# Four sums of blocks of h, made by Pool instead of VectorE

## The chip, the cores and the metric

One core of a Trainium2 chip runs the whole program. The metric is the time of one execution on the device in microseconds (us), as the median of several runs. Engines are named as in the profile: PE is TensorE, PEld its weight loads, DVE is VectorE, ACT is ScalarE, POOL is GpSimd (called Pool here), SP is SyncE, which here issues most of the DMAs.

## What is computed

The reference normalizes x (2048 tokens by 1024), and adds to x a convolution along the hidden dimension (the S4 part) and a gated feed-forward with 4-bit weights. Cut to the part that the change lies in:

```python
xn = layernorm(x)
g = einsum('bsh,ih->bsi', xn, dequantize(gate_Wq, gate_scale, gate_zero))
u = einsum('bsh,ih->bsi', xn, dequantize(up_Wq, up_scale, up_zero))
h = silu(g) * u                       # 2048 tokens x 2752
ffn = einsum('bsi,hi->bsh', h, dequantize(down_Wq, down_scale, down_zero))
out = x + s4(xn) + ffn
```

Each int4 weight is a nibble minus a zero, times a scale, with one zero and one scale for each 64 inputs.

## The kernel before

The matrix products are made by a scheme of the Strassen-Winograd kind: a 2 by 2 block product takes 7 smaller products instead of 8, for sums and differences of blocks that VectorE makes beforehand. Each fp32 operand is split into a high and a low fp16 half, and a product has three passes over these halves (`PASS`, line 530).

The program has three stages.

**Start, up to about 165 us.** x is loaded and normalized token tile by token tile (`norm_stat`, `norm_hi`, `norm_lo`), the blocks of x are combined (`combine`), and the first two of 21 tiles of the inner dimension (j = 0 and 1, 128 rows each) are multiplied plainly (`gate_up_plain`). Many steps of VectorE, ScalarE and SP are pinned here: they run in the order in which they are written (class `Engine`, line 66).

**Gate/up products, to about 888 us.** For j = 2 to 20 and two halves of the tokens (`cp`), `gate_up` makes seven products of 12 matmuls of 512 columns into the PSUM banks A, B, C and D. In between, ScalarE and VectorE evacuate banks: `hb` is C copied and later D added (line 599), `ha` is C copied and B added (lines 602 to 606). Two of the seven products of a group are put off into the next group (`pending`). At the end of `third`, `finish_h` is called with `ha` and `hb`, the blocks of h for the two token halves in `cp`.

Beside these products run two more flows. `load_w` makes the weights of a later j: SP loads `raw` and `sz`, VectorE unpacks the nibbles into `w`, Pool prepares scales and offsets (`scale_c`, lines 290 to 295, three small instructions), ScalarE scales 64 columns at a time, VectorE makes sums (`sums`), ScalarE and VectorE write the high and low fp16 halves into `nat`, and SP transposes `nat` into `wf`, which the matmuls read. `load_wd` does the like for the down weights and stores them to DRAM in seven combinations (`nd` to `WD`), with scales fetched from `SZT`. A smaller flow computes the S4 kernel (tiles `s4n`, `s4p`).

**Convolution and down product, to the end.** The last stage reads the blocks of h (`HF`) and of the down weights (`WD`) from DRAM and multiplies them (line 1187). It is not touched by the change.

`finish_h` is where the change is. For an even j it stores `ha` to `HF[0]` and keeps both tiles as s0 and s2 in `slots`. For the odd j that follows it stores `ha` and `hb` as s1 and s3, and makes four sums of [128 x 512] fp32 tiles in SBUF: s4 = s0 − s2, then s2 = s2 + s3, s0 = s2 − s0, and s6 = s1 − s0. Each is stored to its place in `HF` by a DMA that SP issues (`emit`, line 642). In the trace the tile names are those at allocation, so that s0 and s1 are `ha`, s2 and s3 are `hb`, and s4 and s6 are `s` (for j = 0 and 1, `h` in place of `ha` and `hb`). There are 10 odd j below 20 and two values of `cp`, so 20 calls make 80 sums. The tiles come from the pool "h" (4 buffers under the tag "h" for odd j, 4 under "e" for even j), and a buffer is free again when the DMA that reads it has landed.

The order on each engine comes from two sources. Where a step is pinned, from the code:

```python
            if self.last is None:
                self.last = method(*args, **kw)
            else:
                with self.tc.issue_after(self.last.ins):
                    self.last = method(*args, **kw)
```

Elsewhere a planner (`schedule_with_timeline_sim=True`, line 1370) simulates the program with its own estimates of times, and fixes the order of each engine's instructions by them, and the places of the waits. `G`, Pool's handle, is never pinned (line 115). On the chip each engine and SP's queue issue in the order so fixed.

Of the kernel before, what the change touches and what calls it, by code (L numbers as in the profile page):

```python
# [29 lines left out]
ALU = mybir.AluOpType  # L30
# [57 lines left out]
def build(nc, tc, x, xp, raw_d, sz_d, par_d, vct_d, tab_d, csrow_d, out):  # L88
# [3 lines left out]
    with es:  # L92
# [15 lines left out]
        def htile(name, tag="h"):  # L108
            return pools["h"].tile([P, 512], F32, tag=tag, name=name)
# [4 lines left out]
        V, A = Engine(tc, nc.vector), Engine(tc, nc.scalar)  # L114
        SP, G, PE = Engine(tc, nc.sync), nc.gpsimd, nc.tensor
# [18 lines left out]
        def wtemp(kind, shape, dtype, name):  # L134
            return home[kind].tile(shape, dtype, tag=kind, name=name, **({"bufs": szbufs[0]} if kind == "sz" else {}))
# [14 lines left out]
        def split(dst, src):  # L150

            A.copy(dst[:, 0], src)
            V.tensor_tensor(dst[:, 1], src, dst[:, 0], ALU.subtract)
# [104 lines left out]
        with ea:  # L258
# [11 lines left out]
            def unpack(gi):  # L270

                if gi in FETCH:
                    with tc.issue_after(rs[FETCH[gi], 0].ins):
                        rawt[gi] = load_raw(gi)
                raw, sz = load_raw(gi) if gi not in rawt else rawt.pop(gi)
                w = wtemp("w", [P, 7, 256], F32, f"w{gi}")
                wv = w.rearrange("p a b -> p (a b)")[:, 0:1024]
                q = wv.bitcast(I32).rearrange("p (a b c) -> p a b c", a=16, b=2)
                V.tensor_scalar(q[:, :, 0, :], raw, 4, 15, ALU.logical_shift_right, ALU.bitwise_and)
                V.tensor_scalar(q[:, :, 1, :], raw, 15, None, ALU.bitwise_and)  # L280
                return w, sz
# [280 lines left out]
            def gate_up(j, cp, wf):  # L562
# [46 lines left out]
                def third(ha):  # L609
                    prod(3, bD, False, True)  # L610
                    A.activation(bD, bD, AF.Silu, scale=isc)
                    V.scalar_tensor_tensor(hb, hb, HS * isc, bD, mult, mult)
                    finish_h(j, cp, ha, hb)
# [20 lines left out]
            def finish_h(j, cp, ha, hb):  # L634
                nm = f"{j}_{cp}"
                if j == NJ - 1:
                    for c, h in enumerate((ha, hb)):
                        pc = wtemp("nat", [P, 2, 512], F16, f"hpl{nm}_{c}")
                        split(pc, h)
                        A.dma_start(HPL[cp][:, c, 0:2, :], pc)  # L640
                    return
                def emit(f, src):
                    SP.dma_start(HF[cp][f, :, j // 2, :], src)

                if j % 2 == 0:
                    emit(0, ha)
                    slots[cp] = (ha, hb)
                    return
                s0, s2 = slots.pop(cp)
                s1, s3 = ha, hb  # L650
                s4, s6 = (htile(f"s{n}_{nm}") for n in (4, 6))
                emit(1, s1)
                emit(3, s3)
                V.tensor_tensor(s4, s0, s2, ALU.subtract)
                emit(4, s4)
                V.tensor_tensor(s2, s2, s3, ALU.add)
                emit(2, s2)
                V.tensor_tensor(s0, s2, s0, ALU.subtract)
                emit(5, s0)
                V.tensor_tensor(s6, s1, s0, ALU.subtract)  # L660
                emit(6, s6)


# [171 lines left out]
            w0, s0 = unpack(0)  # L835
            w1, s1 = unpack(1)
# [25 lines left out]
            w2, s2 = unpack(2)  # L862
# [12 lines left out]
            w3, s3 = unpack(3)  # L875
# [41 lines left out]
            h1a = gate_up_plain(1, 0, 0, wt[1])  # L917
            mix_h(0, 1, mix(0, 1))
            finish_h(0, 0, h0a, gate_up_plain(0, 0, 1, wt[0]))
            norms("H8", "S9", "L8", "H9", "S10", "L9", "H10", "S11", "L10", "H11", "S12", "L11")  # L920
            fetch(13)
# [9 lines left out]
            run(t0, 1)  # L931
            norms("L15")
            finish_h(1, 0, h1a, gate_up_plain(1, 0, 1, wt[1]))
            run(t0)
            keep_x(0)
# [438 lines left out]
```

## Time and profile before

| | |
|---|---|
| median of 3 runs | 1339.83 us (1339.01 to 1342.43) |
| the profiled execution | 1342.33 us, span 1340.6 us |
| mean granted TensorE clock in it | 0.989 |
| busy: PE, DVE, ACT, POOL | 1267.3, 992.3, 664.6, 193.1 us |
| the four sums in the stage of gate/up products (190 to 870 us) | 72 instructions, 49.4 us on DVE |

The span runs from the first to the last instruction of the profiled execution; its own time has some 1.7 us more around it. A line of a group gives the line of the kernel, the engine, the operation, the tiles written and read, their shapes, the count, then the busy time in us and the mean of one in ns, and after the bar the idle time of the engine just before them with what ended it. L77 and L82 are lines of the helper that issues most instructions, so that instructions are told apart by their tiles. A line of waits gives who waited for whom, the total in us, how many times, and the longest. A row of the timeline gives the start, the duration, the engine and the instruction; rows of several merged instructions end in their count.

### The profile page before, as it was taken

How to read it: one execution, taken by the hardware profiler on the slowest of the kernel's cores; microseconds unless marked ns; L12 is line 12 of the kernel's file. 1: busy time of each engine (PE TensorE's matmuls, PEld its weight loads, DVE VectorE, ACT ScalarE, POOL GpSimd, SP SyncE). 2: the span in 40 equal slices, each digit the busy share in tenths (PEclk: the TensorE clock that was granted, in tenths of full speed). 3: DMA queues.
4: the chain of work that ended last, by engine and by line, in shares of the span. 5: the costliest groups of instructions: out<-in, count | busy, mean ns of one | idle time of the engine just before them, and what ended most of it. 6: DMA issues, size and time to landing. Idle time of an engine off the chain costs nothing.

```text
span 1340.6 us, 20432 instructions
## 1 busy us (share of the span) xinstructions
PE 1267.3 (95%) x7664; PEld 739.2 (55%) x7664; DVE 992.3 (74%) x1337; ACT 664.6 (50%) x1183; POOL 193.1 (14%) x262
## 2 busy tenths in 40 slices
PE   3799999999989998989989999999999999999998
PEld 3344444444434444434434444455567888888887
DVE  7579966487788769687868776653738897788792
ACT  5468457655736475576648646620204433443330
POOL 4320001000010001000100100000000022255540
PEclk9899999999999999999989999999999999999999
DMA  9993967487799797969869994966837679799991
GB/s 228 210 240 93 195 169 158 104 206 215 181 252 224 175 226 185 266 140 280 221 172 230 209 272 106 242 208 201 332 127 293 247 201 273 246 258 266 288 188 51
DMA packets 377279, 280.72 MB, mean 209 GB/s; under 512 B 230548, under 2 KB 323548, under 8 KB 373084
## 3 DMA queue, kind: packets, MB, share of 16 engines
q1 hardware_dynamic: 354556, 266.31, 72.8%
q0 software_dynamic: 21760, 10.49, 6.6%
q10 hardware_dynamic: 864, 2.62, 0.5%
q8 instruction: 60, 0.98, 0.3%
q14 instruction: 39, 0.32, 0.1%
HBM read 132.36 MB, written 94.84 MB: 169 GB/s over the span
## 4 chain that ended last, share of the span: by engine, by line
PE 40%; DVE 6%; DMA 4%; ACT 2%; issue 2%; SPq 1%; DVEq 0%; ACTq 0%
PE A L1187 14%; PE D L1187 7%; PE cv L1091 5%; PE E L1187 3%; PE cv L1113 3%; DVE w L77 2%; PE D L569 2%; PE A L569 2%; DMA w<-SZT 2%; PE C L569 2%; SPq L77 1%; PE B L569 1%; ACT w L77 1%; PE cc L1126 1%; DMA raw<-qn 1%
## 5 line engine op out<-in xcount | busy, mean ns | idle before, releaser
L569 PEld LDWEIGHTS <-wf 128*128 128x128 f16 x3192 | 313.3, 98 | 418.9 <-issue 43.0
L1187 PEld LDWEIGHTS <-g 128*128 128x128 f16 x2940 | 287.6, 98 | 33.5 <-issue 0.2
L77 ACT ACTIVATE w<-w,sz 128x64 f32<-128x64 int32 x640 | 217.3, 427 | 70.6 <-DVE w L77 66.5
L569 PE MATMUL D<-x,wf 128*128 128x512 f16 x912 | 215.9, 385 | 16.4 <-DVE hb L77 11.9
L569 PE MATMUL A<-x,wf 128*128 128x512 f16 x912 | 213.4, 381 | 10.8 <-DMA wf<-nat 5.5
L569 PE MATMUL C<-x,wf 128*128 128x512 f16 x912 | 207.8, 379 | 2.8 <-DVE ha L77 1.5
L77 ACT CAST g<-a 128x2560 f16<-128x2560 f32 x42 | 97.5, 2324 | 183.2 <-PE cv L1113 53.5
L77 DVE TENSOR_TENSOR w<-w 128x256 f32<-128x256 f32 (+2 forms) x272 | 139.5, 528 | 64.7 <-ACT w L77 56.0
L1187 PE MATMUL A<-b,g 128*128 128x256 f16 x1680 | 185.9, 273 | 0.0
L77 DVE TENSOR_TENSOR g<-a,g 128x2560 f16<-128x2560 f32 x42 | 118.4, 2821 | 30.9 <-ACT g L77 30.9
L1226 POOL DMA_DIRECT2D out<-o x64 | 78.8, 2183 | 340.0 <-DVE o L77 329.7
L292 POOL TENSOR_SCALAR sz<-sz 128x16 f32<-128x16 f32 x41 | 18.5, 451 | 680.8 <-DMA sz<-in_sz 658.5
L569 PE MATMUL B<-x,wf 128*128 128x512 f16 x456 | 107.2, 385 | 2.1 <-ACT B L77 2.1
L538 PEld LDWEIGHTS <-wf 128*128 128x128 f16 x624 | 58.3, 107 | 89.5 <-DMA wf<-natp 30.6
L77 ACT CAST nat<-w 128x896 f16<-128x896 f32 x76 | 68.2, 935 | 72.8 <-issue 51.9
L1187 PE MATMUL D<-b,g 128*128 128x256 f16 x840 | 94.0, 273 | 0.0
L77 DVE TENSOR_TENSOR nat<-w,nat 128x896 f16<-128x896 f32 x76 | 80.3, 1086 | 13.9 <-ACT nat L77 13.8
L77 ACT CAST nd<-w 128x896 f16<-128x896 f32 x70 | 63.3, 935 | 45.6 <-DVE w L77 29.0
L538 PE MATMUL g<-x,wf 128*128 128x512 f16 (+1 forms) x264 | 49.0, 348 | 31.5 <-DMA wf<-natp 27.9
L77 DVE TENSOR_TENSOR nd<-w,nd 128x896 f16<-128x896 f32 x70 | 74.8, 1084 | 2.4 <-ACT nd L77 2.3
L1091 PEld LDWEIGHTS <-x 128*128 128x128 f16 x576 | 52.7, 98 | 25.5 <-issue 4.3
L77 DVE SCALAR_TENSOR_TENSOR p<-cv,p 128x512 f32<-128x512 f32 x32 | 21.9, 689 | 50.5 <-PE cv L1113 45.5
(144 smaller groups left out, 1243.5 us busy)
## 6 DMA issues: line engine op xcount, KB each, us to landing
a<-HF SPq DMA_DIRECT2D x28, 1280.0 KB, 7.9
WD<-nd SPq DMA_DIRECT2D x70, 448.0 KB, 4.2
b<-WD SPq DMA_DIRECT2D x49, 640.0 KB, 6.2
w<-SZT SPq DMA_DIRECT2D x80, 256.0 KB, 5.8
raw<-in_raw SPq DMA_DIRECT2D x65, 256.0 KB, 3.4
HF<-ha SPq DMA_DIRECT2D x54, 256.0 KB, 3.0
HF<-s SPq DMA_DIRECT2D x40, 256.0 KB, 3.2
HF<-hb SPq DMA_DIRECT2D x36, 256.0 KB, 2.6
```

The costliest lines, as they stand in the source:

```text
L77: return method(*args, **kw)
L292: G.tensor_scalar(sz[:, 0], sz[:, 0], WS, None, ALU.mult)
L538: PE.matmul(ps[:, ts], w(k, wi), xt[k // 4][:, xi, k % 4, ts], start=(k == 0 and n == 0), stop=(k == 7 and n == 2))
L569: ends[0] = PE.matmul(ps, wf[kt // 2][:, 14 * (kt % 2) + 2 * fa + wi, :], xt[:, xi, kt, :], start=(start and kt == 0 and n == 0), stop=(st ...
L1091: PE.matmul(dst, w, m, start=first[0], stop=False, skip_group_check=True)
L1113: mm = lambda w, m, stop=False: PE.matmul(ps, w, m, start=False, stop=stop, skip_group_check=True)
L1126: PE.matmul(pc[:, 0:256], xs[:, c, xi, k, ts], band[:, bi, 512 - P * k : 768 - P * k], start=(k == 0 and n == 0), stop=(k == 1 and n == 2))
L1187: PE.matmul(dst, g[:, i, hi, ts], b[:, i, :, wi, :], start=(new and q + i + n == 0), stop=(q == 1 and i == half - 1 and n == 2), skip_grou ...
L1226: G.dma_start(dst, o[:, q], accum_op=ALU.add)
```

## The change

The four sums in `finish_h` are issued on Pool (`G`) instead of VectorE (`V`). Their operands, their order in the code and the stores after them stay as they are.

```diff
@@ -651,13 +651,13 @@
                 s4, s6 = (htile(f"s{n}_{nm}") for n in (4, 6))
                 emit(1, s1)
                 emit(3, s3)
-                V.tensor_tensor(s4, s0, s2, ALU.subtract)
+                G.tensor_tensor(s4, s0, s2, ALU.subtract)
                 emit(4, s4)
-                V.tensor_tensor(s2, s2, s3, ALU.add)
+                G.tensor_tensor(s2, s2, s3, ALU.add)
                 emit(2, s2)
-                V.tensor_tensor(s0, s2, s0, ALU.subtract)
+                G.tensor_tensor(s0, s2, s0, ALU.subtract)
                 emit(5, s0)
-                V.tensor_tensor(s6, s1, s0, ALU.subtract)
+                G.tensor_tensor(s6, s1, s0, ALU.subtract)
                 emit(6, s6)
```

## The prediction

> **What bounds the kernel now.** I read the page first, then the stage that the change touches as one window, then TensorE's waits in that window, then VectorE's groups and SP's waits in it, and last single rows of Pool and VectorE side by side.
>
> ```profile
> span 1340.6 us, 20432 instructions
> ...
> PE 1267.3 (95%) x7664; PEld 739.2 (55%) x7664; DVE 992.3 (74%) x1337; ACT 664.6 (50%) x1183; POOL 193.1 (14%) x262
> ```
>
> TensorE is busy for 95% of the span and nobody else is near it. The sums lie in the stage of gate/up products. Its steady part, 190 to 870 us, as one window (the columns are PE, PEld, DVE, ACT, POOL, clock, DMA share, GB/s):
>
> ```profile
> 190.00:870.00 680.00, 647.88 (x2989) 291.21 (x2988) 510.11 (x856) 419.07 (x914) 54.22 (x102) 0.98 0.81 204
> ```
>
> TensorE stands idle for 680 − 647.9 = 32.1 us of it. No change to VectorE's load can bring more than that, while nothing limits what it can cost. VectorE has 75% of the window, Pool 8%. What TensorE's idle time ended on there (total, times, longest; the first fence is matmuls, the second weight loads):
>
> ```profile
> PE D L569 <- DVE hb L77: 11.9, 6, 4.1
> PE A L569 <- DMA wf<-nat: 5.5, 4, 2.6
> ...
> PE A L569 <- DVE ha L77: 1.8, 2, 0.9
> PE C L569 <- DVE ha L77: 1.5, 1, 1.5
> ```
>
> ```profile
> PEld L569 <- DMA wf<-nat: 9.2, 7, 3.0
> ```
>
> So 11.9 + 1.8 + 1.5 = 15.2 us are VectorE's own late evacuations, and 5.5 + 9.2 = 14.7 us are weight tiles that came late through SP's queue, after VectorE had written their low halves. These 29.9 us are what the change can move, either way.
>
> **The change, part by part.** VectorE loses these four groups of the window (count; busy us, mean ns):
>
> ```profile
> L77 DVE TENSOR_TENSOR ha<-hb,ha 128x512 f32<-128x512 f32 x18 | 12.4, 690 | 0.3
> L77 DVE TENSOR_TENSOR s<-ha,ha 128x512 f32<-128x512 f32 x18 | 12.4, 688 | 0.4 <-DMA HF<-s 0.2
> L77 DVE TENSOR_TENSOR s<-ha,hb 128x512 f32<-128x512 f32 x18 | 12.3, 685 | 0.4 <-DMA HF<-ha 0.4
> L77 DVE TENSOR_TENSOR hb<-hb,hb 128x512 f32<-128x512 f32 x18 | 12.3, 685 | 0.1
> ```
>
> That is 72 instructions and 49.4 us. Eight more, of j = 1, run between 94.8 and 164.6 us. VectorE is full there (39.7 of 40 us in 120 to 160), but TensorE is busy for 38.6 of the same 40 and for 40 of the next 40. The products hide VectorE, and I put those eight at nothing; were that cover gone, they are worth at most 8 × 0.69 = 5.5 us.
>
> Pool gains 80 instructions, and no row shows one of them. The nearest are its `TENSOR_TENSOR` over 16 columns (0.223 us at the median), its `TENSOR_SCALAR` over 1 and over 16 columns (0.192 and 0.253 at the least), and VectorE's `TENSOR_TENSOR` over 8 and 512 columns (0.161 and 0.687). The lower end is 0.22 us, since a wider tile takes no less. If all of it went by column, it would be 32 × 0.223 = 7.1 us. The slope of the two `TENSOR_SCALAR` rows, 4.1 ns a column, gives 0.19 + 511 × 0.0041 = 2.3 us. VectorE's 0.687 times 0.223/0.161 gives 0.95 us. I take 1.2 us, near the last, which compares an operation with its like, while the slope lies between two different scalar operations. [...]
>
> The question is whether a sum on Pool leaves VectorE alone. Two pairs of rows bear on it. The first fence is Pool, the second VectorE (start, duration):
>
> ```profile
> 46.37 0.22 POOL L293 TENSOR_TENSOR sz<-sz 128x16 f32<-128x16 f32 x1
> 46.68 0.25 POOL L294 TENSOR_SCALAR sz<-sz 128x16 f32<-128x16 f32 x1
> ...
> 47.53 1.24 POOL L181 TENSOR_SCALAR rs<-mv 128x1 f32<-128x1 f32 x1
> ```
>
> ```profile
> 46.03 1.28 DVE L82 BATCH_NORM_STATS2 st<-n 128x6 f32<-128x512 f32 x2
> 47.41 0.21 DVE L82 BATCH_NORM_AGGREGATE mv<-st 128x2 f32<-128x12 f32 x1
> 47.54 1.17 DVE L82 TENSOR_TENSOR n<-n 128x1024 f16<-128x1024 f32 x1
> ```
>
> Beside `bn_stats`, which reads one tensor, Pool's small operations take their usual 0.22 and 0.25 us. Beside a `TENSOR_TENSOR`, which reads two tensors from SBUF, one that needs 0.19 takes 1.24 and ends when the other does. At 393.04 us another takes 2.07: a row of two-tensor operations runs on VectorE until 394.91, where `hb<-D,hb` begins, which has only one input in SBUF. So Pool waits for VectorE's two-tensor operations. The averages of the three groups of `scale_c` over their least times (0.451, 0.448, 0.575 over 0.253, 0.222, 0.253 us) say how long: 0.25 us for one.
>
> The reverse, VectorE waiting for Pool, is not in this trace, because Pool's operations are too short to show it. Its bounds are nothing and the whole 1.2 us. I take the whole: what one engine waits for until the other's instruction ends is held, not divided. [...]
>
> The sum for VectorE: Pool's 72 operations last 72 × 1.2 = 86 us. After the change VectorE is busy for 510.1 − 49.4 = 460.7 us. The four evacuations that read PSUM (24.0 + 23.9 + 23.8 + 23.8 = 95.5 us by their rows) do not collide. The other 365 us, 54% of the window, do. 86 × 0.54 = 47 us are lost to holding, against 49.4 gained. I enter zero. With 0 held it is −49.4 us; with 2.3 us for one, 166 × 0.54 − 49.4 = +40.
>
> To turn VectorE's load into TensorE's time I let the 29.9 us of waits go as load/(1 − load), an assumption. 75% gives 3.0; 68% (460.7 us) gives 2.1, or 9 us less; 81% (550 us) gives 4.3, or 13 us more.
>
> Next SP's queue. All four sums of a pair are followed by a store to HF on SP (`emit`), and SP issues in order, so a late sum holds up what is queued behind its store: WD stores, raw loads, and the transposes that make `wf`. SP waits in this way already (total, times, longest):
>
> ```profile
> SPq L77 <- DVE s L77: 19.7, 22, 3.9
> SPq L77 <- DVE hb L77: 19.2, 20, 2.8
> ```
>
> A sum on Pool is 1.2 + 0.25 − 0.69 = 0.76 us later than on VectorE. `s2`, `s0` and `s6` depend on each other, so the last store comes 2.3 us late, 41 us over 18 pairs. 68 transposes `wf<-nat` lie in the window, and TensorE waited for 4 + 7 = 11 of them, one in six. So a sixth of the 41 us, 7 us, reaches TensorE. The ends are nothing, if every transpose is ordered ahead of the late stores, and 17 us with 2.3 us on Pool (1.86 × 3 × 18 / 6).
>
> Pool's own queue holds `scale_c`, three instructions for each of 34 loads in the window, and ScalarE's scaling of `w` waits for it. A sum that waits there for `hb`, or for a slot of the "h" tiles, delays the `scale_c` behind it. From the end of L294 to the first ACTIVATE on `w`, nine places that I read have from 0.5 to about 7 us, and ScalarE is free for 261 of the 680 us. I enter nothing; without that cover, one sum in front of each is 34 × 1.45 = 49 us of ScalarE waiting, a sixth of it 8 us.
>
> Together: 1342.3 us, the profiled execution's own time (span 1340.6 and 1.7 around it), + 0 + 7 = 1349.3. That execution stood 2.5 above the median of the three runs, 1339.8, so on the median's footing it is 1347.
>
> **The rivals.** First, *faster*: Pool's sums do not hold VectorE, its load falls to 68%, and SP's lateness is hidden. −9 us gives 1331; even with all 29.9 us gone it is 1310. For it speaks that the sums no longer queue among VectorE's work, and `s4`, which needs only the even block, can run early. Against it: Pool's stretched rows. It decides if VectorE's rows keep 0.42 and 1.08 us beside Pool's sums.
>
> Second, *no change*: VectorE even, and SP's lateness within the waits that it has anyway (114.3 us on `w` alone). 1340.
>
> Third, *much slower*: a sum takes 2.3 us alone. VectorE at 81% and SP give 13 + 17 = 30 us, 1370. It decides from about 1.5 us on Pool upwards. The 1.24 us for one column speaks for waiting, not for slow work, and so against it.
>
> The order of each engine's instructions outside the pinned parts comes from a planner that estimates times, and with other costs it lays them anew. No row prices that. Its bounds are the 32.1 us that TensorE idles in the window, shifted either way; a third, 10 us, widens each case.
>
> **How the numbers follow.** The forecast, 1347, has 0.40; its own range is 1343 to 1358. Faster has 0.28, no change 0.20, much slower 0.12. About 0.3%, 4 us, is what a measurement of this kernel can tell from no change. Faster by more than that: 0.28. Within it: 0.20. Slower: 0.40 + 0.12 = 0.52. The range goes from 1330, just under the faster rival's 1331 (about a tenth lies below it), to 1366, short of the slow rival's 1370 (about a tenth lies above).
>
> **What would show it.** Right: VectorE's group counts fall by 80 while its two-tensor rows grow longer (a mean of `w<-w` 128x256 above 0.42 us, of `nat` above 1.09), or its busy time in the stage falls by much less than 49 us; Pool's new rows last about 1.2 to 1.5 us; SP waits for Pool's `s`, `ha`, `hb`; TensorE's idle time in the stage grows from 32 to about 39 us, on `wf<-nat`. Wrong: VectorE's rows keep their lengths and TensorE's wait for `hb` shrinks (the first rival), or Pool's rows are over 2 us (the third).

## The result, and the profile after

| | median us | runs | ratio to before (95%) |
|---|---|---|---|
| before | 1339.42 | 4 (1338.52 to 1342.43) | |
| after | 1360.38 | 4 (1358.89 to 1361.03) | 1.0164 (1.0151 to 1.0178) |

The change costs 21 us. The forecast was 1347, with 1330 to 1366 as its range: the direction was right, and the loss is three times the 7 us that were forecast. 1360 lies within the wide range, but above the 1343 to 1358 that belonged to the forecast itself. The profiled execution after the change took 1361.03 us. Its page:

```profile
span 1359.2 us, 20491 instructions
...
PE 1273.3 (94%) x7664; PEld 738.7 (54%) x7664; DVE 999.1 (74%) x1257; ACT 663.5 (49%) x1183; POOL 308.6 (23%) x342
```

VectorE has 80 instructions fewer and is busy for 6.8 us longer (992.3 before). Pool is busy for 115.5 us more. TensorE executes the same 7664 matmuls and is busy for 6.0 us longer. The first matmul of the gate/up stage starts at 150.9 us (148.2 before), and the stage ends some 19 us later than before; behind it the two traces run alike (of the last 452 us TensorE is busy for 446.5 before and for 446.6 after). So some 16 us of the loss lie in the stage of the change and 2.7 us ahead of it. The window of the stage, with the columns as in the prediction (PE, PEld, DVE, ACT, POOL, clock, DMA share, GB/s):

```profile
190.00:870.00 680.00, 637.99 (x2919) 285.88 (x2918) 506.72 (x777) 409.39 (x894) 144.94 (x168) 0.98 0.79 198
```

TensorE stands idle for 42.0 us of 680 in place of 32.1 and gets 2919 matmuls done in place of 2989. VectorE's load hardly moves (506.7 for 510.1). What TensorE waited for there:

```profile
PE D L569 <- DVE hb L77: 15.8, 7, 3.3
PE D L569 <- ACT D L77: 14.6, 6, 4.9
PE B L569 <- ACT B L77: 7.6, 3, 4.4
PE C L569 <- DVE ha L77: 2.1, 1, 2.1
```

The waits for evacuations, VectorE's and ScalarE's, grow. Of ScalarE's, these were there before the change:

```profile
PE D L569 <- ACT D L77: 4.5, 3, 3.9
PE B L569 <- ACT B L77: 2.1, 1, 2.1
```

The waits for `wf<-nat`, before the change 5.5 us of matmuls and 9.2 of weight loads, are gone. SP waits little for Pool:

```profile
SPq L77 <- POOL s L660: 6.0, 6, 1.8
SPq L77 <- POOL ha L658: 3.1, 5, 1.0
...
SPq L77 <- POOL hb L656: 2.8, 5, 0.9
SPq L77 <- POOL s L654: 2.7, 2, 1.4
```

Pool's groups, the sums alone (72 of the 80):

```profile
L654 POOL TENSOR_TENSOR s<-ha,hb 128x512 f32<-128x512 f32 x18 | 28.7, 1595 | 10.5 <-DVE hb L77 9.0 <-issue 1.0
L658 POOL TENSOR_TENSOR ha<-hb,ha 128x512 f32<-128x512 f32 x18 | 27.0, 1502 | 1.3
L656 POOL TENSOR_TENSOR hb<-hb,hb 128x512 f32<-128x512 f32 x18 | 26.8, 1487 | 135.7 <-DVE hb L77 124.2 <-issue 11.6
L660 POOL TENSOR_TENSOR s<-ha,ha 128x512 f32<-128x512 f32 x18 | 26.5, 1471 | 5.2 <-DVE ha L77 2.0 <-DVE w L77 2.0
```

A sum takes 1.47 to 1.60 us on the mean. Where none has to wait it takes 1.26, as the first two rows of the next fence show. The timeline, Pool in the first fence and VectorE in the second:

```profile
707.17 1.26 POOL L656 TENSOR_TENSOR hb<-hb,hb 128x512 f32<-128x512 f32 x1 [0.52 <-DVE hb L77]
708.51 1.26 POOL L658 TENSOR_TENSOR ha<-hb,ha 128x512 f32<-128x512 f32 x1
709.85 2.15 POOL L660 TENSOR_TENSOR s<-ha,ha 128x512 f32<-128x512 f32 x1
712.09 2.13 POOL L654 TENSOR_TENSOR s<-ha,hb 128x512 f32<-128x512 f32 x1
```

```profile
709.67 1.21 DVE L77 TENSOR_TENSOR w<-raw,w 128x1024 f32<-128x1024 int16 x1
710.91 2.17 DVE L77 TENSOR_TENSOR w<-w 128x1024 f32<-128x1024 f32 x1
713.01 1.82 DVE L77 TENSOR_SCALAR qn<-raw 128x512 int16<-128x512 int16 x2
```

This is the holding, from both sides. L660 starts at 709.85, while `w<-raw,w` is at work until 710.88, and ends at 712.00, 1.12 us after that. The next VectorE instruction, `w<-w`, ends at 713.08, 1.08 us after L660; it takes 2.17 us, and one like it takes 1.23 in the trace of before. L654, next on Pool, ends at 714.22, 1.14 us after `w<-w`. The two engines take turns. Two instructions that would take 1.26 and 1.23 alone stretch to over 2 us where they meet. Held instructions show here as longer rows (2.15 and 2.17 us), not as idle time in front of them. VectorE's groups in the window after the change:

```profile
L77 DVE TENSOR_TENSOR w<-w 128x256 f32<-128x256 f32 x216 | 103.1, 488 | 67.0 <-ACT w L77 64.2
L77 DVE TENSOR_TENSOR nd<-w,nd 128x896 f16<-128x896 f32 x70 | 83.1, 1205 | 3.4 <-ACT nd L77 3.3
...
L77 DVE TENSOR_SCALAR w<-raw 128x512 int32<-128x512 int32 x69 | 31.3, 493 | 0.5
...
L77 DVE TENSOR_TENSOR hb<-D,hb 128x512 f32<-128x512 f32 x33 | 22.6, 685 | 23.6 <-PE D L569 23.5
```

The same groups before the change:

```profile
L77 DVE TENSOR_TENSOR w<-w 128x256 f32<-128x256 f32 x216 | 87.8, 421 | 58.3 <-ACT w L77 56.0
L77 DVE TENSOR_TENSOR nd<-w,nd 128x896 f16<-128x896 f32 x70 | 74.8, 1084 | 2.4 <-ACT nd L77 2.3
...
L77 DVE TENSOR_SCALAR w<-raw 128x512 int32<-128x512 int32 x70 | 26.5, 418 | 0.2
...
L77 DVE TENSOR_TENSOR hb<-D,hb 128x512 f32<-128x512 f32 x35 | 24.0, 685 | 11.2 <-PE D L569 11.2
```

Groups with two inputs in SBUF grow, `w<-w` from 421 to 488 ns, `nd<-w,nd` from 1084 to 1205 and `nat<-w,nat` from 1086 to 1129, but not every one: `w<-raw,w` 128x1024 takes 1218 for 1220. And it is not only these: `w<-raw`, a `TENSOR_SCALAR` with a single input tensor, grows from 418 to 493. `hb<-D,hb`, which has one input in PSUM, stays at 685.

### The profile page after: what moved, and what is told of

It reads as the page before. It is cut to its first block, busy times and chain, and to the rows that moved or that the text cites. A ratio compares the mean times of both kernels' runs of the same rounds, so it can differ in the third digit from the quotient of the medians.

```text
span 1359.2 us, 20491 instructions
## 1 busy us (share of the span) xinstructions
PE 1273.3 (94%) x7664; PEld 738.7 (54%) x7664; DVE 999.1 (74%) x1257; ACT 663.5 (49%) x1183; POOL 308.6 (23%) x342
## 5 line engine op out<-in xcount | busy, mean ns | idle before, releaser
L569 PE MATMUL D<-x,wf 128*128 128x512 f16 x912 | 219.2, 390 | 31.2 <-DVE hb L77 16.7
L77 DVE TENSOR_TENSOR w<-w 128x256 f32<-128x256 f32 (+2 forms) x272 | 161.1, 603 | 77.7 <-ACT w L77 64.2
L569 PE MATMUL A<-x,wf 128*128 128x512 f16 x912 | 208.8, 379 | 0.5 <-DVE ha L77 0.5
L77 DVE TENSOR_TENSOR nat<-w,nat 128x896 f16<-128x896 f32 x76 | 83.9, 1137 | 17.4 <-ACT nat L77 17.4
L77 DVE TENSOR_TENSOR nd<-w,nd 128x896 f16<-128x896 f32 x70 | 83.1, 1205 | 3.4 <-ACT nd L77 3.3
L538 PE MATMUL g<-x,wf 128*128 128x512 f16 (+1 forms) x264 | 45.7, 330 | 28.0 <-DMA wf<-natp 25.2
```

The source lines that it names most:

```text
L77: return method(*args, **kw)
L538: PE.matmul(ps[:, ts], w(k, wi), xt[k // 4][:, xi, k % 4, ts], start=(k == 0 and n == 0), stop=(k == 7 and n == 2))
L569: ends[0] = PE.matmul(ps, wf[kt // 2][:, 14 * (kt % 2) + 2 * fa + wi, :], xt[:, xi, kt, :], start=(start and kt == 0 and n == 0), stop=(st ...
```

## The experiments

The planner lays every engine's order anew, so after differs from before in far more than the sums. In the kernels below, the order of the instructions of TensorE, VectorE, ScalarE and SP is therefore fixed as the planner had it before ("old order") or after ("new order") the change. Pool's order is left to the planner, except in dve_new_order. The diffs are shortened: what records the instructions and fixes their order is left out. A "held" time below is how much longer VectorE is busy than its own instructions make it; where the sums are on Pool, that is its busy time less the 944.8 us of short_old_order. Ratios are to runs of the kernel before on the same chip, with intervals of 95%, and differences in us are differences of ratios times 1340 us.

### The change taken apart: order, relief, load

pool_old_order: the change, in the old order. dve_new_order: VectorE's sums, in the new order, which fixes Pool too; the places of the sums themselves are the planner's. short_old_order and short_new_order: Pool's sums over 16 of 512 columns, the rest left out.

```diff
-                V.tensor_tensor(s4, s0, s2, ALU.subtract)
+                G.memset(s4, 0.0); G.tensor_tensor(s4[:, 0:16], s0[:, 0:16], s2[:, 0:16], ALU.subtract)
...
+                # likewise s2, s0 and s6, without a fill where the tile is written already
```

> The sums run on Pool as in the change, but PE, DVE, ACT and SP are held to the exact order that they had before (DVE without the sums). Theory A (holding: Pool's sums keep VectorE's two-tensor operations waiting, which makes its evacuations and weight halves late): the order does not matter, 1354 to 1364 us, with VectorE's rows stretched by some 50 us in total. Rival B (order: the planner, seeing other costs, laid the queues in a worse order): 1336 to 1346 us. Rival C (late stores: a sum on Pool ends later, and SP's queue stands behind its store): over 1364, since in the old order the stores are placed for VectorE's times; SP's waits on Pool's tiles over 30 us.

Measured: 1357.13 us, 1.0130 (1.0109 to 1.0151).

> The sums are back on VectorE, but PE, ACT, SP and Pool stand in the order of the changed kernel, and so do VectorE's other operations; the sums are put among them by the planner. Theory A (holding): as fast as the kernel before, 1336 to 1346 us. Rival B (order): 1352 to 1364 us, as slow as the changed kernel. Rival C (late stores): 1336 to 1346.

Measured: 1344.27 us, 1.0033 (1.0020 to 1.0046).

> As the first, in the order of before, but each of Pool's sums reads and writes only 16 of the 512 columns; the rest of the sums is left out (s4 and s6 are filled with zeros by Pool, which only writes). VectorE loses its 80 sums and is held for almost nothing. Theory A: as fast as before or faster, 1326 to 1340 us; the distance to the first run is the price of holding. Rival B: as before, 1335 to 1342. Rival C: the sums' ends are early again, so as before.

Measured: 1330.75 us, 0.9933 (0.9916 to 0.9949).

> The 16-column sums of short_old_order, with PE, DVE, ACT and SP in the order of the changed kernel. If order and holding simply add: 1335 us (1330.8 + 4.4), 1332 to 1338, and the changed kernel's 21 us are then 26 of holding, 4 of order and 9 of relief. If the new order suits a VectorE without the sums (which it was laid for): 1326 to 1331.

Measured: 1338.65 us, 0.9988 (0.9975 to 1.0000).

The order is worth 0.33%, 4.4 us, with VectorE's sums, and as much with Pool's (1.0164 less 1.0130); with short sums it is 7. It is the smaller part. The sums on Pool bring 17 us without it. And the relief of VectorE is small: with nearly nothing left of the sums on either engine, the kernel gains 0.67%, 9.0 us. The page and the window of short_old_order:

```profile
PE 1263.2 (95%) x7664; PEld 736.3 (56%) x7664; DVE 944.8 (71%) x1257; ACT 665.1 (50%) x1183; POOL 248.0 (19%) x382
```

```profile
190.00:870.00 680.00, 656.23 (x3038) 295.75 (x3037) 466.25 (x782) 419.06 (x912) 97.93 (x207) 0.99 0.82 206
```

VectorE is relieved of 992.3 − 944.8 = 47.5 us, so a microsecond of sums cost 9.0/47.5 = 0.19. That is rather too much, since the short sums also end earlier (see below), and the 9.0 us include what this is worth. TensorE idles for 23.8 us. The same two rows of pool_old_order:

```profile
PE 1273.1 (94%) x7664; PEld 737.9 (54%) x7664; DVE 997.7 (73%) x1257; ACT 663.9 (49%) x1183; POOL 317.3 (23%) x342
```

```profile
190.00:870.00 680.00, 638.37 (x2915) 285.27 (x2914) 505.12 (x776) 410.63 (x897) 157.84 (x170) 0.97 0.79 198
```

VectorE is held for 997.7 − 944.8 = 52.9 us, and TensorE idles for 41.6. Against before, VectorE's load is the same (505.1 and 510.1 in the window) and TensorE loses 9.5 us more of it. 10 of the 26 us between the two kernels are TensorE's own busy time: the same 7664 matmuls take 1273.1 us of it for 1263.2. Their trace shows where most of it comes from. Some matmuls of the stage last up to 0.63 us instead of 0.38, 37 in short_old_order and 72 in pool_old_order (counted from 0.45 us up). All of them start within 5 us after the end of a wait of TensorE, in packets of at most 12, and what they take beyond 0.38 grows from 8.6 to 16.9 us.

### Holding doubled, and one sum alone

both_old_order: VectorE makes the sums, and Pool makes them too into a tile that nobody reads. hold_old_order: before, with four subtractions on Pool that nobody reads for each pair. one_old_order: only s4 on Pool.

```diff
+                idle = cst.tile([P, 512], F16, tag="idle", bufs=1, name=f"idle{nm}")
+                for _ in range(4): G.tensor_tensor(idle, s1, s3, ALU.subtract)   # hold_old_order
                 V.tensor_tensor(s4, s0, s2, ALU.subtract)
```

> The kernel before in its exact order, with its sums on VectorE; Pool makes each sum a second time, into an fp16 tile that nobody reads. No store and no engine waits for Pool's copy. Theory A: only holding is added, on a VectorE that keeps its 55 us of sums: 1360 to 1385 us, more than the change. Rival B: order and waits are as before, 1337 to 1344. Rival C: no store waits for Pool, 1337 to 1344.

Measured: 1379.21 us, 1.0291 (1.0276 to 1.0307). VectorE had to wait for Pool's reads before it could write `ha` and `hb` (13.7 and 7.5 us in the window), so this is not holding alone.

> The kernel before in its exact order, with its sums on VectorE. For each pair Pool also subtracts s3 from s1 four times into a tile that nobody reads; s1 and s3 are not written again before their buffers are free, so that VectorE waits for no result of Pool and no store does. Theory A: holding alone on top of the full VectorE: 1360 to 1376 us, with VectorE busy for 1035 to 1050 us. Rival C: 1338 to 1344.

Measured: 1378.37 us, 1.0292 (1.0264 to 1.0321), a little above the range that was expected. VectorE is busy for 1062.0 us, 69.7 more than before: 39.1/69.7 = 0.56 us of time for one that is held.

> In the order of before, only s4 = s0 - s2 is made by Pool, the other three sums by VectorE. It is the sum that hangs on nothing of its own pair. Theory A, if the price goes by the number of sums: a quarter of the 17 us of pool_old_order, 1342 to 1346 us. If it comes from the runs of three sums in a row on Pool: 1336 to 1341.

Measured: 1343.22 us, 1.0022 (1.0011 to 1.0033). Even the sum that nothing on Pool waits for loses; the time lies in the range for a price by the number of sums.

### Lateness: a run that did not test it, and one that did

late_old_order has sums over 16 columns and fills that only write, meant to make them as long as whole ones.

```diff
+                G.tensor_tensor(s2[:, 0:16], s2[:, 0:16], s3[:, 0:16], ALU.add)
+                for _ in range(2): G.memset(s2[:, 16:512], 0.0)
```

> In the order of before, each sum on Pool is made of 16 columns and two zero fills of its tile (the other 496 columns of the sums are left out): about 1.4 us long as a real sum on Pool, but for all but a moment it only writes and reads nothing from SBUF. Its stores are as late as those of pool_old_order. Theory A (the price is VectorE being held by Pool's reads): 1328 to 1336 us, like short_old_order, with VectorE busy for some 945 us. Rival C (late stores in SP's queue, late buffers): 1350 to 1360, like pool_old_order. In between, the 26 us between those two runs are shared out by where it falls.

Measured: 1332.7 us, 0.9946 (0.9929 to 0.9964). I read this as "lateness costs 2 us", and the reading fell. The fills touch no column that the next sum reads, and the planner laid them beside the chain. From the end of `hb<-hb,D` to the end of the s6 sum, the mean of the 18 pairs of j = 3 to 19 is 2.3 us here and in short_old_order, 4.5 in before, 5.2 in pool_old_order. Only stores that wait for fills can have been late, and SP's waits for Pool's sums and fills add up to 12.1 us in the window.

Then two kernels that vary one thing each, which with short_old_order and pool_old_order make a table of two by two. In tardy_old_order the fills stand in the chain:

```diff
+                def fill(t): G.memset(t[:, 16:512], 0.0); G.memset(t[:, 16:512], 0.0); G.memset(t[:, 16:272], 0.0)
+                G.tensor_tensor(s2[:, 0:32], s2[:, 0:32], s3[:, 0:32], ALU.add); fill(s2)
+                emit(2, s2); G.tensor_tensor(s0[:, 0:32], s2[:, 0:32], s0[:, 0:32], ALU.subtract); fill(s0)
```

> Lateness without holding: each sum on Pool takes in 32 of its 512 columns only and is followed, in the chain and ahead of its store, by write-only fills of the other columns, so that it lasts about as long as a whole sum. The output is not the reference's. Theory 'lateness' (the 26 us between short_old_order and pool_old_order come from sums that end late, and what waits for them in SP's queue): 1345 to 1357. Rival 'holding' (they come from VectorE being held): 1330 to 1337.

Measured: 1344.27 us, 1.0029 (1.0015 to 1.0043), just under the range of "lateness" and well above that of its rival. The chain, with its fills, ends 7.4 us after `hb<-hb,D`, which is later than in pool_old_order. In shorthold_old_order the short sums come first and the holding behind them:

```diff
+                for _ in range(4): G.tensor_tensor(idle, s1, s3, ALU.subtract)   # ordered behind the 16-column s6
```

> Holding without lateness: the 16-column sums of short_old_order, and behind the fourth of each pair four whole subtractions on Pool that nobody reads. The output is not the reference's. Theory 'holding': VectorE is held for about 45 us and the time is 1348 to 1358. Rival 'lateness': 1330 to 1338.

Measured: 1362.25 us, 1.0168 (1.0138 to 1.0197), above the range that was expected of holding.

| ratio to before | sums end early | sums end late |
|---|---|---|
| VectorE not held | 0.9933 (short_old_order) | 1.0029 (tardy_old_order) |
| VectorE held | 1.0168 (shorthold_old_order) | 1.0130 (pool_old_order) |

Holding with early sums costs 2.35%, 31 us, for 989.4 − 944.8 = 44.6 us held (0.71 for one). It is not quite holding alone: ScalarE's waits for Pool grew as well, from 10.8 us of the window in short_old_order to 24.0, with `scale_c` behind the added subtractions. In pool_old_order they are 9.0 us, so there Pool's queue shows no part in the 26 us. Lateness alone costs 0.96%, 13 us, with these waits at 20.0. Holding and lateness together cost 1.97%, 26 us, not 44: between these two kernels with VectorE held, lateness adds nothing that shows. The windows, of tardy_old_order and then of shorthold_old_order:

```profile
190.00:870.00 680.00, 642.24 (x2962) 288.54 (x2961) 467.80 (x777) 415.15 (x907) 183.85 (x381) 0.98 0.80 201
```

```profile
190.00:870.00 680.00, 639.38 (x2920) 285.97 (x2919) 495.65 (x777) 412.01 (x899) 190.83 (x268) 0.98 0.79 199
```

In the first, Pool is busy for 183.9 us and VectorE for 467.8, nearly as in short_old_order (466.3): fills that only write hold it hardly at all. Its two-input `w<-w` 128x256 stays at 421 ns beside them (420 in short_old_order); of the larger groups only one-input ones grow (`w<-raw` from 425 to 453). In late_old_order, with fills too, it is the same: `w<-w` 420, `nd<-w,nd` 1084 (1085 in short_old_order), `w<-raw` 457. In the second, Pool is hardly busier, and VectorE needs 28 us more for the same instructions. What holds the two-input instructions is Pool's reading: beside it `w<-w` 128x256 takes 448 ns and `nd<-w,nd` 1196, for 420 and 1085 in short_old_order. The lateness of the first shows in SP's waits (`L654` is there the line of the fills):

```profile
SPq L77 <- POOL s L654: 31.2, 23, 4.9
SPq L77 <- POOL ha L654: 16.5, 11, 4.6
```

These are 47.7 us, where after has 14.6 for all its sums. So 13 us is the price of a lateness greater than that of the change: 5.1 us more at the end of the chain than in short_old_order. pool_old_order ends its chain 0.7 us later than before; in proportion, an estimate from these two runs, that is 2 of its 17 us.

### Other ways to lessen it

gate_old_order: every sum on Pool may begin only when the VectorE instruction that stood ahead of it in the old order has ended. split_old_order: each sum as four instructions of 128 columns. gap_old_order: 36 sums on Pool (the expectation says 38), each tied behind a VectorE instruction that a gap followed in the trace of short_old_order. poolstore_old_order: the stores of the sums on Pool's queue.

```diff
+            tc.add_manual_dep(pool_sum, vector_instruction_ahead, Sync)               # gate, gap
+                for c in QUARTERS: G.tensor_tensor(s4[:, c], s0[:, c], s2[:, c], ALU.subtract)   # split
+                G.tensor_tensor(s4, s0, s2, ALU.subtract); G.dma_start(HF[cp][4, :, j // 2, :], s4)   # poolstore
```

> The four sums on Pool as in pool_old_order and in the same order of the other engines, but each sum may begin only when the VectorE instruction that stood just ahead of it in the order of before has ended. Theory 'place' (a held microsecond costs more than a removed one because Pool's sums begin as soon as their inputs are there, in front of VectorE's evacuations, while VectorE's own sums stood in the order where they delayed nothing): the holds fall where the sums fell before, and the time is 1343 to 1351, against 1357 for pool_old_order. Rival 'amount' (only the number of held microseconds counts, wherever they fall): 1354 to 1362.

Measured: 1352.04 us, 1.0091 (1.0075 to 1.0107), between the two ranges. VectorE is held for 984.1 − 944.8 = 39.3 us in place of 52.9. Fewer held microseconds, at much the same price.

> As pool_old_order, with each sum on Pool made by four instructions of 128 columns in place of one of 512. Theory 'length of one hold' (an evacuation is delayed because it stands behind a single long Pool instruction): no hold is longer than some 0.4 us, and the time falls to 1340 to 1350. Rival 'amount' (Pool's whole time beside VectorE's two-input operations counts): 80 sums take as long or longer in four parts, and the time is 1357 or more.

Measured: 1367.78 us, 1.0218 (1.0190 to 1.0245). "Length of one hold" falls. VectorE is held for 30 us only, but four parts take 2.5 to 2.9 us together, and the s6 sum ends 8.3 us after `hb`: the lateness is greater. Here 38 us above short_old_order stand against 30 held, so a lateness of this size seems to count beside holding too; no run separates the two.

> 38 of the 80 sums on Pool, the other 42 on VectorE in the order of before; each of the 38 is tied to begin after a VectorE instruction that a gap of at least 1.1 us followed in the trace of short_old_order. Theory 'place': the 38 hold little, VectorE loses 38 x 0.69 = 26 us, about half of what short_old_order loses for 9 us, and the time is 1333 to 1340. Rival 'amount': 38 of 80 parts of pool_old_order's 17 us, 1345 to 1351.

Measured: 1348.85 us, 1.0066 (1.0048 to 1.0085), inside the range of "amount", but not for its reason. Pool's sums there:

```profile
L654 POOL TENSOR_TENSOR s<-ha,hb 128x512 f32<-128x512 f32 x10 | 12.7, 1267 | 66.5 <-DVE hb L77 17.8 <-DVE ha L77 15.0 <-DVE nat L77 14.6
L658 POOL TENSOR_TENSOR ha<-hb,ha 128x512 f32<-128x512 f32 x7 | 8.9, 1267 | 0.6
```

1267 ns is the time of a sum that does not wait (the s6 sums, with 1311, wait a little), and VectorE's 970.9 us are 21.4 fewer than before, which is 36 times the 0.59 that a removed sum is worth (47.5/80): the holding is gone. The s6 sums end 6.0 us after `hb`. So sums that hold nobody, but wait for their gaps, still lose 9 us; what the tying itself adds was not measured apart.

> pool_old_order with the stores of the four sums issued on Pool's queue instead of SP's, behind the sums themselves. Theory 'lateness', by SP's queue: nothing on SP waits for a sum any more, and the time falls from 1357 to 1335 to 1345. Rival 'holding': 1351 to 1362.

Measured: 1367.16 us, 1.0207 (1.0178 to 1.0237). With nothing on SP waiting for a sum, the kernel is 10 us slower than pool_old_order: nothing of the loss came back with SP's queue free. But a store on Pool's queue takes Pool 0.57 to 0.59 us, the s6 sum ends 6.7 us after `hb`, and VectorE is held for 1004.9 − 944.8 = 60.1 us in place of 52.9. So the run does not show SP's queue by itself.

### VectorE's own time, added

twice_old_order: before, with one more subtraction on VectorE behind each sum, which nobody reads.

```diff
                 V.tensor_tensor(s4, s0, s2, ALU.subtract)
+                V.tensor_tensor(idle, s0, s2, ALU.subtract)
```

> The kernel before with each of VectorE's 80 sums followed by one more of its kind on VectorE that nobody reads: 80 x 0.69 = 55 us more of VectorE's own time, at the sums' places, and nothing held. Theory 'kind' (a microsecond at the sums' places costs about 0.2, as the removed ones saved, and it is the held ones that are dear): 1348 to 1355. Rival 'curve' (VectorE's time gets dearer as its load grows, whoever causes it): 0.5 for each, 1362 to 1375.

Measured: 1360.18 us, 1.0157 (1.0129 to 1.0185), between the two ranges. 21.0 us for 1040.8 − 992.3 = 48.5 us more of VectorE: 0.43 for one. So an added microsecond costs more than a removed one saves, even at the same places, and a held one (0.50 to 0.71) is dearer still, or as dear.

## Why the prediction went wrong, step by step

**Held against removed, entered as zero: the step that failed.** I sized the holding at 47 us for 72 sums (86 × 0.54 is 46); pool_old_order shows 52.9 for 80, as much for each, and VectorE's busy time came out even, as said. But I set 47 held against 49.4 removed and entered zero, as if each microsecond had the same price. The removed ones were worth 0.19 each (9.0 us in all), the held ones 0.50 (26 us), each with the sums' earlier or later end in it. The net is 17 us, with the load unchanged; some 2 us of it go to lateness by the estimate above. A conversion by load/(1 − load) cannot give it, since it sees only the total.

**The conversion itself.** For the relief it gave 9 us, and short_old_order measured 9.0, which is partly luck. Its base of 29.9 us counts the weights twice: the weight loads' 9.2 us of waits are the same stretches as the matmuls' 5.5 (both stand at 216.3, 224.0, 453.8 and 576.4 us). TensorE's 32.1 us of idle time were VectorE's 15.2, 5.5 for `wf` and 11.2 for ScalarE's evacuations, which the prediction left out and which grew most, to 23.7 in after. From 20.7 us the conversion gives 6. It also left out that TensorE's busy time is not fixed: 10 of the 26 us are there, most of it in the slow matmuls behind waits. The first rival, 1331, is what short_old_order shows without holding; the change cannot have it, because Pool's sums read and hold VectorE, for 52.9 us in pool_old_order.

**SP's late stores, 7 us.** The chain was late by less than I wrote: it ends 5.1 us after `hb` for 4.5 in before, so 0.6 late in place of 2.3. The 4 + 7 waits for `wf` held the same events twice, so it was 7 transposes in 68 and not one in six. In after, SP waits for the sums 14.6 us in all, and TensorE no longer waits for `wf<-nat`, where the 7 us were to appear. A much greater lateness alone costs 13 us. The term sat in the wrong place.

**Pool's own queue, entered as nothing.** In after, ScalarE waits 16.5 us for `scale_c` in the window, four times, and not at all before. What that cost was not measured; in the old order it shows no part, as ScalarE's waits for Pool are 9.0 us in pool_old_order and 10.8 in short_old_order.

**The planner, no price, ±10.** It is +4.4 us.

**The price of a sum on Pool.** Taken as 1.2 us alone and 1.45 with waiting; measured 1.26 and 1.47 to 1.60. The third rival's condition, 2.3 us alone, did not come. Its 1370 was near because the holding costs more, not because the sums are slow.

**What the sums are worth on VectorE.** 49.4 us by their rows, but VectorE's busy time fell by 43.9 in the window (510.1 to 466.3), and by 0.59 for each of the 80 sums over the whole program: rows that follow each other directly overlap by some 0.09 us, 0.687 less 0.59 (`ha<-hb,ha` ends at 715.06 us in the trace of before, and `hb<-D,hb` behind it starts at 714.98).

**The start, nothing.** The gate/up stage begins 2.7 us later, within the 5.5 us that were given as the price without cover.

**Who holds whom.** No row of before showed VectorE waiting for Pool; that it waits for the whole of a Pool instruction was my choice between two bounds, and the trace of after has it so. Beside a sum on Pool, which reads, `w<-w` 128x1024 with its two SBUF inputs ended 1.08 us after the sum and took 2.17 us for 1.23, and the mean of `w<-w` 128x256 went from 421 to 488 ns. Beside fills, which only write, it did not grow: 421 ns in tardy_old_order and 420 in late_old_order, for 420 in short_old_order.

So the loss is −0.67% for the relief, +1.97% for holding with lateness, and +0.33% for the order: 1.63%, of the 1.64% measured. The first two add up to pool_old_order's 1.30% by the way they are taken; that the order's share comes on top is the one thing that this sum tests.

**Open.** Why a held microsecond costs 0.5 to 0.7 where one added at the sums' places costs 0.43 and a removed one saves 0.19. Pool's sums come three in a row behind `hb`, so VectorE may lose several microseconds at once; no run here shows whether that is the reason, nor by which way lateness costs its 13 us when it is alone. Which waits are followed by slow matmuls stays open as well: gap_old_order idles for 42.4 us of the window and has 40 of them, pool_old_order for 41.6 and has 72. No kernel that makes the whole sums beat the one before.

## What to carry to other kernels

Before moving work to Pool, look whether it reads SBUF while VectorE runs two-input instructions from SBUF (`w<-w` grew from 421 to 488 ns here), and look at VectorE's one-input rows too (`w<-raw` grew from 418 to 493); if so, put the sum of Pool's time beside such instructions next to the time removed. Do not set the two against each other one for one: here removed time was worth 0.19 and held time cost 0.50 to 0.71. To price an engine's relief, shrink the work to almost nothing in a fixed order and run that; to test lateness, look in the trace that the chain really ended late.

## What the runs showed that I had not expected

- Two stretched rows can stand side by side: a sum of 1.26 us alone took 2.15, and the VectorE instruction behind it 2.17 for 1.23.
- TensorE's busy time for the same 7664 matmuls went from 1263.2 us (short_old_order) over 1267.3 (before) to 1273.1 (pool_old_order) and 1276.3 (twice_old_order), while its mean granted clock in the window fell from 0.99 to 0.97. It does not simply follow the idle time: gap_old_order idles for 42.4 us of the window, and its matmuls take 1265.7.
- The order that the planner laid for VectorE's sums is better than the one that it laid for Pool's, even when the sums are nearly nothing (0.9933 and 0.9988).
